# Reordering the head and the normalisation step of a one-core attention kernel: first chunk's copies on ScalarE, other first loads, zeros multiplied on TensorE

## The chip, the cores and the metric

The kernel runs on one core of a Trainium2 chip. The metric is the time of one execution on the device in microseconds (us). Engines are named as in the profile: PE (TensorE matmuls), PEld (its weight loads), DVE (VectorE), ACT (ScalarE), POOL (GpSimd), SP (SyncE, which only issues DMAs here). Lines such as L506 are lines of the kernel before; the changed kernel has its own numbers, about ten higher.

## What is computed

Four sequences of 1024 tokens with 512 features go through a layer norm, an attention with a local window and a compressed sparse part, and a quantised product with a second weight, which is added. In outline:

```
x   = layernorm(hidden)                       # 4 x 1024 x 512
q   = rope(rmsnorm(x @ Wq + bq))              # 16 heads of 128
lk  = rope(rmsnorm(x @ Wlk + blk)),  lv = x @ Wlv + blv
ent = softmax over groups of 4 tokens (x @ Wcmp) weights x     # 256 entries a sequence
ck  = rope(rmsnorm(ent @ Wk + bk)),  cv = ent @ Wv + bv
window part:  softmax(q . lk) over the last 128 tokens, times lv
sparse part:  softmax over the 8 best of q . ck (causal), times cv
out = hidden + (window + sparse) @ Wo + bo + quantised(x) @ quantised(input2)
```

Everything outside the quantised product is in float32.

## The kernel before

**Tiling.** Tokens are handled in 32 chunks of 128, eight to a sequence. A chunk meets the heads in eight units of two heads. So there are 256 units, numbered n = 8 t + u for chunk t and unit u.

**Pipeline.** The main loop goes over slots s. In slot s, PE does the scores of unit s, the query and key products of unit s+3 (`queries`, L478: qp), the output product of s-2 (L797), the values product of s+1 (L581: vp), and the context of s-1 (L764: cp). VectorE and ScalarE do the softmaxes of unit s: `weigh` (DVE L649 to L655 finds the row maxima and the 8 best; ACT L656 and L664 take exponentials), `settle` (DVE L671, L680, L681, L682 masks the sparse part and scales it) and `settle_window` (ACT L687 scales the window part). `normalize(s+2)` (DVE L506, four instructions a unit: th) applies the rms norm to queries and keys; it is the last to read qp, so it frees that PSUM buffer. `squares` (ACT L318) and `spread` (POOL L312, L313: r) make the norm's factor for s+3.

**Rotation.** `rotate` is a generator: POOL's rb product (L332) and DVE's product (L333), then at the second call DVE's subtraction and addition (L335, L336). `normalize` starts it, and `end_rotation` finishes it.

**Two ways to transpose.** From unit 8 on, keys and probabilities are turned by DVE (L556, L559, L705) and a round trip through DRAM (SP issues: qk, qT, lkT, pr, probT; L747 fetches probT in four DMAs). In chunk 0 and for the last unit, PE transposes (tq L534, tp L728), and the results are copied from PSUM: keys by `keep_keys` (ACT L540, DVE L541), probabilities by `keep_turned` (L736: the first of two on ACT, the second on DVE).

**Chunk preparation.** `chunk_prep(t)` is another generator, stepped through labels (A0, B0, A1, ... B7): layer norm (bn_stats on DVE L353, centring on ACT L363, xn on DVE L369), transposes (PE L373), the entries' products (PE L386 yp, L416 ep), their norm (ACT junk_e, POOL er, DVE L437) and rotation (rb_e on POOL; DVE L335, L336), and ck's transpose. For later chunks one label is taken at each `steps()`; the entries are normalised and rotated in unit 5. For chunk 0 the loop drives it by `until` in the slots before slot 0. In chunk 0 too, `fold_first_row` (DVE L269) folds the biases into the weights, and the second weight is quantised in three passes a step.

**Order.** The schedule is written out by hand: each engine executes its instructions in the order of the calls below, and waits where a semaphore says so. qp has a ring of two PSUM buffers of its own; vp, tq, tp, xp, yp, ep and fp share another of two ("pp"). DMAs issued by SP and ACT count on eight completion semaphores in turn, so one waits for the DMA eight before it.

Of the kernel before, what the change touches and what calls it, by code (L numbers as in the profile page):

```python
# [12 lines left out]
F32 = mybir.dt.float32  # L13
# [6 lines left out]
P = 128  # L20
# [18 lines left out]
def kernel(  # L39
# [58 lines left out]
    def load_x(t, purpose):  # L98

        b, c = divmod(t, NCH)  # L100
        xt = work.tile([P, HID], F32, tag="x", name=f"x_{purpose}_{t}")
        nc.sync.dma_start(xt, hidden[b, ts(c, P), :])
        x_tiles[purpose, t] = xt
# [26 lines left out]
    def load_wo(u, engine):  # L130
        engine.dma_start(wo_sb[u], Wo[ts(u, 256), :].rearrange("(h p) n -> p h n", p=P))

    load_x(0, "norm")
    load_wqk(0, nc.sync)
    load_x(1, "norm")
    load_angles(0)

    wkv_sb = const.tile([P, KK, 2 * D + 1], F32, name="wkv_sb")
    nc.sync.dma_start(wkv_sb[:, :, 0:D], Wk.rearrange("(k p) n -> p k n", p=P))
    nc.sync.dma_start(wkv_sb[:, :, D : 2 * D], Wv.rearrange("(k p) n -> p k n", p=P))  # L140
    load_wlv(0, nc.sync)
    load_wqk(1, nc.sync)
    load_angles(1)
    load_wlv(1, nc.sync)
    load_wqk(2, nc.sync)
    load_wlv(2, nc.sync)


    with nc.allow_non_contiguous_dma(reason="512 words once"):
        nc.scalar.dma_start(  # L150
            wkv_sb[:, :, 2 * D : 2 * D + 1], Wcmp.rearrange("(k p) o -> p k o", p=P)
        )
    bias_f = work.tile([P, 1024], F32, tag="probT", name="bias_f", bufs=1)[0:BLK, 0:512]
    nc.vector.memset(bias_f, 0.0)
    nc.scalar.dma_start(bias_f[0:NU, 0:256], bq.rearrange("(u n) -> u n", u=NU))
    nc.scalar.dma_start(bias_f[0:NU, 256:512], blk.rearrange("(u n) -> u n", u=NU))
    bkv_sb = const.tile([NE, 2 * D], F32, name="bkv_sb")
    nc.scalar.dma_start(bkv_sb[:, 0:D], bk.partition_broadcast(NE))
    nc.scalar.dma_start(bkv_sb[:, D : 2 * D], bv.partition_broadcast(NE))
    norm_w = const.tile([P, 2, D], F32, name="norm_w")  # L160
    nc.scalar.dma_start(norm_w[:, 0, :], qn_w.partition_broadcast(P))
    nc.scalar.dma_start(norm_w[:, 1, :], kn_w.partition_broadcast(P))
    blv_n = work.tile([P, 2, P], F32, tag="cT", name="blv_n", bufs=1)[0:NH, 0, :]
    nc.scalar.dma_start(blv_n, blv.rearrange("(h d) -> h d", h=NH))
    bcmp_sb = const.tile([P, 1], F32, name="bcmp_sb")
    nc.scalar.dma_start(bcmp_sb, bcmp.partition_broadcast(P))
    scales = const.tile([P, 2], F32, name="scales")
    nc.scalar.dma_start(scales[:, 0:1], scale.partition_broadcast(P))
    nc.scalar.dma_start(scales[:, 1:2], scale1.partition_broadcast(P))


    nhalf = const.tile([P, 4], F32, name="nhalf")
    nc.vector.memset(nhalf, -0.5)

# [4 lines left out]
    make_identity(nc, ident)  # L179
    ident_b = const.tile([P, P], BF16, name="ident_b")  # L180
    inv = const.tile([P, 1], F32, name="inv")
    bias_b = const.tile([P, 512], BF16, name="bias_b")
    nc.vector.memset(bias_b, 0.0)
    sel = const.tile([P, NU], BF16, name="sel")
    mask_b = const.tile([P, 2 * P + NE], BF16, name="mask_b")
    bo_sb = const.tile([P, HID], F32, name="bo_sb")
# [133 lines left out]
    def rotate(th, cs, nh, a, name):  # L320

        p = th.shape[0]
        a = a.rearrange("p (h t f) -> p h t f", h=nh, t=2)
        bb = work.tile([p, nh, 2, HALF], F32, tag=f"ropeb{nh}", name=f"rb_{name}", bufs=1)
        x12 = th[:, :, 0:ROPE].rearrange("p h (t f) -> p h t f", t=2)

        def wide(v):
            return v.unsqueeze(1).unsqueeze(1).to_broadcast([p, nh, 2, HALF])  # L330

        nc.gpsimd.tensor_tensor(bb, x12, wide(cs[:, HALF:ROPE]), ALU.mult)  # L332
        nc.vector.tensor_tensor(a, x12, wide(cs[:, 0:HALF]), ALU.mult)  # L333
        yield
        nc.vector.tensor_tensor(x12[:, :, 0, :], a[:, :, 0, :], bb[:, :, 1, :], ALU.subtract)  # L335
        nc.vector.tensor_tensor(x12[:, :, 1, :], a[:, :, 1, :], bb[:, :, 0, :], ALU.add)  # L336
# [5 lines left out]
    def chunk_prep(t):  # L342
# [14 lines left out]
        if c == 0:  # L357
            nc.gpsimd.memset(cv, 0.0)
        yield "B0"

        off = work.tile([P, 2], F32, tag="off", name=f"off_{t}")
        nc.gpsimd.tensor_scalar(off[:, 0:1], st[:, 6:7], -1.0, None, ALU.mult)
        nc.scalar.activation(  # L363
            xt, xt, AF.Identity, bias=off[:, 0:1], scale=1.0, accum_out=off[:, 1:2]
        )
        nc.gpsimd.tensor_scalar(off[:, 1:2], off[:, 1:2], 1.0 / HID, None, ALU.mult)
        yield "A1"
        xn = scratch(f"xn_{t}")
        nc.vector.tensor_scalar(xn, xt, off[:, 1:2], r, ALU.subtract, ALU.mult)  # L369
        yield "B1"  # L370
        xp = pp(f"xp_{t}")
        for k in range(KK):
# [128 lines left out]
    def normalize(n):  # L501
# [15 lines left out]
        next(w["rotation"])  # L517
        w["th"], w["thb"] = th, thb

    def end_rotation(n):  # L520
        for _ in units[n].pop("rotation"):
            pass
# [13 lines left out]
    def keep_keys(n):  # L536
        w = units[n]
        tq = w.pop("tq").rearrange("p (t g a i) -> p t g a i", t=2, g=2, a=NB)
        qT, lkT = key_tiles(n)
        nc.scalar.copy(qT.rearrange("p a (i g) -> p g a i", g=2), tq[:, 0])  # L540
        nc.vector.tensor_copy(lkT.rearrange("p a (g i) -> p g a i", g=2), tq[:, 1])  # L541

    def key_tiles(n):
        w = units[n]
# [186 lines left out]
    def keep_turned(n):  # L731
        w, g = units[n], len(parts_of(n))
        probT = work.tile([P, 1024], F32, tag="probT", name=f"probT_{n}", bufs=1)
        probT = of_heads(probT, n)
        for h, tp in enumerate(w.pop("tp")):
            (nc.vector.tensor_copy if h else nc.scalar.copy)(  # L736
                probT[:, :, ds(h * g, g), :],
                tp.rearrange("p (g a i) -> p a g i", a=NB, i=BLK),
            )
        w["probT"] = probT  # L740
# [81 lines left out]
    def for_unit(n, *todo):  # L822
        if 0 <= n < NN:
            for f, *more in todo:
                f(n, *more)

    first, rounding = chunk_prep(0), round_w2()
    until(first, "A1")
    nc.vector.tensor_copy(ident_b, ident)
# [5 lines left out]
    for s in range(-3, NN + 2):  # L835
        t, u = place(s)

        if s == -2 or u == 7 and 0 <= t and t + 2 < NT:
            running = [*running[-2:], chunk_prep(t + 2)]
        if u == 3 and 0 <= t < NT:  # L840
            load_x(t, "sum")
        if u == 6 and 0 <= t < NT:
            running = [*running[-2:], chunk_eight(t)]
        if u == 4 and 0 <= t and t + 2 < NT:
            load_x(t + 2, "norm")

        for_unit(s, (scores, 0), (scores, 1))
        for_unit(s - 2, (keep_context,))
        for_unit(s, (weigh, 0), (weigh, 1))
        for_unit(s + 3, (queries,))  # L850
        if s + 1 < NU:
            for_unit(s + 1, (turn_keys_here,))
        for_unit(s, (settle, 0), (settle, 1))
        for_unit(s, (settle_window, 0), (settle_window, 1))
        for_unit(s + 2, (normalize,))
        if by_dma(s):
            turn(s)
        if s < 0:
            until(first, ("B3", "B4", "B6")[s + 3])
        steps()  # L860
        for_unit(s + 3, (squares, (0, 1, 2, 3)), (spread,))
        if s + 1 < NU:
            for_unit(s + 1, (keep_keys,))
        for_unit(s - 2, (to_output,))
        steps()
        for_unit(s + 2, (end_rotation,))
        if s + 2 >= NU:
            for_unit(s + 2, (turn_keys,))
        if s == -1:
            until(first, "B7")  # L870
        for_unit(s + 1, (values_of,))
        if not by_dma(s):
            for_unit(s, (turn_here,))
        for_unit(s - 1, (values,))
        if by_dma(s):
            fetch(s)
        else:
            for_unit(s, (keep_turned,))
        if s + 2 >= NU:
            for_unit(s + 2, (fetch_keys,))  # L880
        for_unit(s + 1, (keep_values,))

        if 0 <= s < NU:
            fold_first_row(s)
        if 0 <= s + 1 < NU:
            load_first_row(s + 1)
        if s < NU:

            if s == -1:
                late_constants()  # L890
                for k in range(KK):
                    nc.scalar.dma_start(w2_raw[k], input2[ts(k, P), :])
            if 0 <= s < KK:
                for _ in range(4):
                    next(rounding, None)
            if 3 <= s + 6 < NU:
                load_wqk(s + 6, nc.scalar)
            if 3 <= s + 4 < NU:
                load_wlv(s + 4, nc.scalar)
            if 0 <= s + 1 < NU:  # L900
                load_wo(s + 1, nc.scalar)
        if u == 6 and 0 <= t and t + 2 < NT:
            load_angles(t + 2)
        units.pop(s - 1 - NU, None)
# [46 lines left out]
```

## Time and profile before

| What | Value |
|---|---|
| Time, median of 3 runs | 2800.16 us (2798.2 to 2800.68) |
| Time of the profiled execution | 2798.32 us |
| Span of the profiled execution | 2796.6 us |
| Granted TensorE clock, mean | 0.994 |
| PE busy | 2735.4 us (98%) |
| DVE, ACT, POOL busy | 2263.3, 1345.1, 842.6 us |
| First scores (slot 0) | 44.25 us |
| Scores of slot 8 | 157.79 us |

The profile is of one execution. The span runs from its first to its last instruction, and the execution's own time lies 1.7 us above it. An engine's busy time is the union of its instructions. The page cuts the span into 40 slices, with a digit for tenths busy. The lists of waits say which engine, at which line, waited, for whom, for how long in all, how many times, and the longest. In rows of instructions, three durations stand as minimum, median and maximum in ns. The letters before and after `<-` are the tiles written and read.

### The profile page before, as it was taken

Reading aid. Unit: us, or ns where it says so; the run is one execution under the profiler, and the core shown is the slowest. Engines: PE = TensorE matmul, PEld = TensorE weight load, DVE = VectorE, ACT = ScalarE, POOL = GpSimd, SP = SyncE. Lnnn points to the kernel's source line nnn. Section 1 sums busy time; section 2 is a strip of 40 time slices with the busy share of each in tenths; the row PEclk is TensorE's granted clock in tenths of the full one; section 3 lists DMA queues with packets and bytes.
Section 4 is the critical chain, followed back from the end, with each engine's and each line's share of the span. In section 5 each row is a group of like instructions: output and inputs, shape, how many; then the busy total and the mean of one; then the engine's idle time right before and its main releaser. Section 6 shows DMA issues by size and latency. Waiting matters only on the chain.

```text
span 2796.6 us, 48466 instructions
## 1 busy us (share of the span) xinstructions
PE 2735.4 (98%) x12721; PEld 1856.4 (66%) x12721; DVE 2263.3 (81%) x9171; ACT 1345.1 (48%) x5170; POOL 842.6 (30%) x1225
## 2 busy tenths in 40 slices
PE   5799999999999999999999999999999999999998
PEld 3566666676666666666666666666666666666765
DVE  4687888888877788888888787888888878888886
ACT  2345544445455554444445455454444545544443
POOL 2333332233332333322233322333223333222321
PEclk9899999999999999999999999999999999999999
DMA  6345445555544545555554454555555444455554
GB/s 203 98 119 139 136 136 155 154 154 154 146 125 139 139 141 141 154 152 152 153 142 134 132 140 138 152 155 145 153 149 143 129 139 139 136 152 161 145 150 125
DMA packets 623187, 401.96 MB, mean 144 GB/s; under 512 B 307152, under 2 KB 576320, under 8 KB 622912
## 3 DMA queue, kind: packets, MB, share of 16 engines
q1 hardware_dynamic: 610688, 385.29, 50.2%
q10 hardware_dynamic: 12224, 13.56, 1.6%
q8 instruction: 104, 1.70, 0.3%
q14 instruction: 171, 1.40, 0.2%
HBM read 214.64 MB, written 184.03 MB: 143 GB/s over the span
## 4 chain that ended last, share of the span: by engine, by line
PE 92%; DVE 2%; DMA 1%; issue 0%; SPq 0%; ACT 0%; POOL 0%; DVEq 0%; ACTq 0%; POOLq 0%
PE qp L478 30%; PE op L797 15%; PE vp L581 15%; PE cp L764 14%; PE sc L626 5%; PE sc L616 4%; PE sc L623 4%; PE yp L386 2%; PE fp L458 1%; PE ep L416 1%; PE xp L373 0%; DVE wqk L269 0%; DMA probT<-pr 0%; PE sc L627 0%; DVE th L506 0%
## 5 line engine op out<-in xcount | busy, mean ns | idle before, releaser
L478 PE MATMUL qp<-wqk,xnT 128*128 128x512 f32 x2048 | 944.7, 604 | 2.8 <-issue 2.1
L332 POOL TENSOR_TENSOR rb<-th,cs 128x256 f32<-128x256 f32 x256 | 248.1, 969 | 1673.7 <-DVE th L506 1673.7
L478 PEld LDWEIGHTS qp<-wqk,xnT 128*128 128x128 f32 x2048 | 370.3, 191 | 382.9 <-issue 371.7
L581 PEld LDWEIGHTS vp<-wlv,xnT 128*128 128x128 f32 x2048 | 393.0, 192 | 181.6 <-issue 115.8
L581 PE MATMUL vp<-wlv,xnT 128*128 128x256 f32 x2048 | 490.9, 383 | 17.9 <-DVE lkT L541 13.6
L656 ACT ACTIVATE prob<-sc,neg 128x256 f32<-128x256 f32 (+1 forms) x512 | 235.6, 460 | 550.9 <-DVE taken L655 540.4
L797 PE MATMUL op<-wo,cT 128*128 128x512 f32 x1024 | 488.0, 599 | 0.5 <-ACT cT L779 0.5
L649 DVE CUSTOM_DVE_ANT_0 sc<-sc,mask_b 128x256 f32<-128x256 f32 (+1 forms) x512 | 208.0, 406 | 279.8 <-PE sc L627 279.6
L593 ACT COPY lv<-vp 128x256 f32<-128x256 f32 x256 | 95.2, 372 | 471.6 <-PE cp L764 412.7
L687 ACT ACTIVATE prob<-prob,tot 128x256 f32<-128x256 f32 (+1 forms) x512 | 252.4, 493 | 129.1 <-DVE tot L681 127.8
L797 PEld LDWEIGHTS op<-wo,cT 128*128 128x128 f32 x1024 | 186.4, 190 | 189.4 <-issue 129.2
L764 PE MATMUL cp<-probT,lv 128*128 128x128 f32 x1920 | 300.7, 277 | 6.3 <-DMA probT<-pr 5.7
L318 ACT ACTIVATE junk<-qp 128x128 bf16<-128x128 f32 x1024 | 279.7, 273 | 33.1 <-PE qp L478 5.0
L506 DVE SCALAR_TENSOR_TENSOR th<-qp,r,norm_w 128x128 f32<-128x128 f32 x1024 | 286.8, 343 | 5.7 <-ACT junk L318 3.2
L764 PEld LDWEIGHTS cp<-probT,lv 128*128 128x128 f32 x1920 | 275.5, 193 | 23.4 <-issue 10.3
L705 DVE STREAM_TRANSPOSE probB<-prob 128x512 f32<-128x512 f32 (+2 forms) x494 | 281.9, 608 | 0.0
L313 POOL TENSOR_TENSOR r<-r,nhalf 128x4 f32<-128x4 f32 x256 | 260.5, 1018 | 21.3
L764 PE MATMUL cp<-probT,cv 128*128 128x128 f32 x1536 | 257.1, 277 | 0.0
L626 PE MATMUL sc<-ckT,qT 128*128 128x96 f32 (+7 forms) x1024 | 226.3, 303 | 0.0
L764 PEld LDWEIGHTS cp<-probT,cv 128*128 128x128 f32 x1536 | 214.8, 194 | 0.0
L623 PE MATMUL sc<-lkT,qT 128*128 128x128 f32 x1024 | 207.9, 285 | 0.0
L779 ACT ACTIVATE cT<-cp,blvT 128x128 f32<-128x128 f32 x512 | 160.0, 364 | 92.7 <-PE cp L764 83.4
(130 smaller groups left out, 3802.1 us busy)
## 6 DMA issues: line engine op xcount, KB each, us to landing
pr<-probB SPq DMA_DIRECT2D x127, 512.0 KB, 2.6
probT<-pr SPq DMA_DIRECT2D x508, 128.0 KB, 2.9
qk<-thb SPq DMA_DIRECT2D x992, 64.0 KB, 1.8
pr<-probB SPq DMA_DIRECT2D x96, 384.0 KB, 2.3
probT<-pr SPq DMA_DIRECT2D x384, 96.0 KB, 2.4
qT<-qk SPq DMA_DIRECT2D x248, 128.0 KB, 2.9
lkT<-qk SPq DMA_DIRECT2D x248, 128.0 KB, 2.8
x_norm<-_attn_hidden_states_dram SPq DMA_DIRECT2D x32, 256.0 KB, 3.0
```

The lines of the kernel that those rows point to most:

```text
L313: nc.gpsimd.tensor_tensor(r, r, nhalf[: ss.shape[0], 0:n], ALU.pow)
L318: nc.scalar.activation(junk[: src.shape[0]], src, AF.Square, accum_out=acc)
L332: nc.gpsimd.tensor_tensor(bb, x12, wide(cs[:, HALF:ROPE]), ALU.mult)
L478: nc.tensor.matmul(qp, xnT[:, k if k or not t else KK, :], wqk_sb[u][:, k, :], start=(k == 0), stop=(t > 0 and k == KK - 1),)
L506: nc.vector.scalar_tensor_tensor(th[:, i, :], qp[:, ts(i, D)], r[:, i : i + 1], norm_w[:, i // 2, :], ALU.mult, ALU.mult,)
L581: nc.tensor.matmul(vp[:, 0:256], xnT[:, k, :], wlv_sb[u][:, k, :], start=(k == 0), stop=(k == KK - 1),)
L623: nc.tensor.matmul(blocks(sc[:, P : 2 * P]), q, lkT[:, :, ds(h * BLK, BLK)], start=True, stop=True)
L626: nc.tensor.matmul(sc[:, spa], q, ckT[:, 0:m], start=True, stop=False)
L687: nc.scalar.mul(prob[:, loc], prob[:, loc], tot[:, 0:1])
L705: nc.vector.transpose(pb[:, :, ds(h * g, g), :], prob[:, parts[0] * P : (parts[-1] + 1) * P].rearrange("p (g b i) -> p b g i", b=NB, i=BLK),)
L764: nc.tensor.matmul(blocks(cp[:, h, :]), v, probT[:, :, h * len(parts) + i - parts[0], :], start=(i == parts[0]), stop=(i == parts[-1]),)
L797: nc.tensor.matmul(op, cT[:, h, :], wo_sb[u][:, h, :], start=(u == 0 and h == 0), stop=(u == NU - 1 and h == 1),)
```

## The change

1. **First loads.** SP's order becomes x0, Wq and Wlk of unit 0, Wk, Wv, Wq and Wlk of unit 1, angles 0, x1, Wq and Wlk of unit 2, three times Wlv, angles 1. ACT's DMAs start with the biases; blv and the two scales are issued in slot -2 (`late_loads`).
2. **First layer norm.** In chunk 0, xn is made on DVE straight from mean and factor; the centring pass on ACT and the two POOL instructions around it remain for later chunks.
3. **Zeros on PE.** Twelve bf16 matmuls of a zero tile (128x128 by 128x512) stand first in PE's queue.
4. **Copies on ACT.** The second copy of keys and that of probabilities in chunk 0 move from DVE to ACT; the probabilities' copy of the last unit too.
5. **Order within a slot.** `normalize(s+2)` moves ahead of `settle` in every slot. Its rotation's POOL product stays with it, and DVE's product of the rotation follows after `settle_window` (`go_on_rotating`). In chunk 0 the keys' transposes move ahead of the queries.
6. **First entries.** In slots -3 to -1 the preparation of chunk 0 is driven further (B3, A6, B6 instead of B3, B4, B6) and placed ahead of `normalize`; in slot -1, vp stands ahead of the last step.

```diff
+    load_x(0, "norm")
+    nc.vector.memset(bias_f, 0.0)
+
+    nc.scalar.dma_start(bias_f[0:NU, 0:256], bq.rearrange("(u n) -> u n", u=NU))
+    nc.scalar.dma_start(bias_f[0:NU, 256:512], blk.rearrange("(u n) -> u n", u=NU))
     load_wqk(0, nc.sync)
-    load_x(1, "norm")
-    load_angles(0)
...
+    load_wqk(1, nc.sync)
+    load_angles(0)
...
+    load_x(1, "norm")
+    load_wqk(2, nc.sync)
+    load_wlv(0, nc.sync)
+    load_wlv(1, nc.sync)
+    load_wlv(2, nc.sync)
+    load_angles(1)
+
+    def late_loads():
+        nc.scalar.dma_start(blv_n, blv.rearrange("(h d) -> h d", h=NH))
+        nc.scalar.dma_start(scales[:, 0:1], scale.partition_broadcast(P))
+        nc.scalar.dma_start(scales[:, 1:2], scale1.partition_broadcast(P))
+
+    bias_b = const.tile([P, 512], BF16, name="bias_b")
+    nc.vector.memset(bias_b, 0.0)
...
         nc.gpsimd.tensor_tensor(bb, x12, wide(cs[:, HALF:ROPE]), ALU.mult)
+        yield
         nc.vector.tensor_tensor(a, x12, wide(cs[:, 0:HALF]), ALU.mult)
         yield
...
+        xn = None
+        if t:
...
+        else:
+            xn = scratch(f"xn_{t}")
+            nc.vector.tensor_scalar(xn, xt, st[:, 6:7], r, ALU.subtract, ALU.mult)
         yield "A1"
...
+    def go_on_rotating(n):
+        next(units[n]["rotation"])
+
...
-        nc.vector.tensor_copy(lkT.rearrange("p a (g i) -> p g a i", g=2), tq[:, 1])
+        nc.scalar.copy(lkT.rearrange("p a (g i) -> p g a i", g=2), tq[:, 1])
...
-            (nc.vector.tensor_copy if h else nc.scalar.copy)(
+            nc.scalar.copy(
...
+    warm = pp("warm")
+    for _ in range(12):
+        nc.tensor.matmul(warm, bias_b[:, 0:P], bias_b, start=True, stop=True)
+
...
         for_unit(s, (weigh, 0), (weigh, 1))
+        if 0 <= s < NU - 1:
+            for_unit(s + 1, (turn_keys_here,))
         for_unit(s + 3, (queries,))
-        if s + 1 < NU:
+        if s < 0:
             for_unit(s + 1, (turn_keys_here,))
+            until(first, ("B3", "A6", "B6")[s + 3])
+        for_unit(s + 2, (normalize,))
         for_unit(s, (settle, 0), (settle, 1))
         for_unit(s, (settle_window, 0), (settle_window, 1))
-        for_unit(s + 2, (normalize,))
+        for_unit(s + 2, (go_on_rotating,))
         if by_dma(s):
             turn(s)
-        if s < 0:
-            until(first, ("B3", "B4", "B6")[s + 3])
         steps()
...
+        for_unit(s + 1, (values_of,))
         if s == -1:
             until(first, "B7")
-        for_unit(s + 1, (values_of,))
...
+            if s == -2:
+                late_loads()
             if s == -1:
                 late_constants()
```

More of the change, by code (lines that the diff above doesn't have):

```diff
@@ L131, in load_wo @@
         engine.dma_start(wo_sb[u], Wo[ts(u, 256), :].rearrange("(h p) n -> p h n", p=P))
+    wkv_sb = const.tile([P, KK, 2 * D + 1], F32, name="wkv_sb")
+    bias_f = work.tile([P, 1024], F32, tag="probT", name="bias_f", bufs=1)[0:BLK, 0:512]
+    bkv_sb = const.tile([NE, 2 * D], F32, name="bkv_sb")
+    norm_w = const.tile([P, 2, D], F32, name="norm_w")
+    bcmp_sb = const.tile([P, 1], F32, name="bcmp_sb")
+    scales = const.tile([P, 2], F32, name="scales")
+    blv_n = work.tile([P, 2, P], F32, tag="cT", name="blv_n", bufs=1)[0:NH, 0, :]
     load_x(0, "norm")
+    nc.vector.memset(bias_f, 0.0)
+    nc.scalar.dma_start(bias_f[0:NU, 0:256], bq.rearrange("(u n) -> u n", u=NU))
+    nc.scalar.dma_start(bias_f[0:NU, 256:512], blk.rearrange("(u n) -> u n", u=NU))
     load_wqk(0, nc.sync)
-    load_x(1, "norm")
-    load_angles(0)
[L138 to L146, printed above, removed]
     with nc.allow_non_contiguous_dma(reason="512 words once"):
@@ L152 @@
         )
[L153 to L157, printed above, removed]
+    nc.sync.dma_start(wkv_sb[:, :, 0:D], Wk.rearrange("(k p) n -> p k n", p=P))
+    nc.sync.dma_start(wkv_sb[:, :, D : 2 * D], Wv.rearrange("(k p) n -> p k n", p=P))
+    nc.scalar.dma_start(norm_w[:, 0, :], qn_w.partition_broadcast(P))
+    nc.scalar.dma_start(norm_w[:, 1, :], kn_w.partition_broadcast(P))
+    nc.scalar.dma_start(bcmp_sb, bcmp.partition_broadcast(P))
+    load_wqk(1, nc.sync)
+    load_angles(0)
     nc.scalar.dma_start(bkv_sb[:, 0:D], bk.partition_broadcast(NE))
     nc.scalar.dma_start(bkv_sb[:, D : 2 * D], bv.partition_broadcast(NE))
[L160 to L169, printed above, removed]
+    load_x(1, "norm")
[10 more added lines that the diff above has]
+    nc.vector.memset(bias_b, 0.0)
     nhalf = const.tile([P, 4], F32, name="nhalf")
@@ L181 @@
     inv = const.tile([P, 1], F32, name="inv")
-    bias_b = const.tile([P, 512], BF16, name="bias_b")
-    nc.vector.memset(bias_b, 0.0)
     sel = const.tile([P, NU], BF16, name="sel")
@@ L359, in chunk_prep @@
         yield "B0"
[L361 to L366, printed above, removed]
+        xn = None
+        if t:
+            off = work.tile([P, 2], F32, tag="off", name=f"off_{t}")
+            nc.gpsimd.tensor_scalar(off[:, 0:1], st[:, 6:7], -1.0, None, ALU.mult)
+            nc.scalar.activation(
+                xt, xt, AF.Identity, bias=off[:, 0:1], scale=1.0, accum_out=off[:, 1:2]
+            )
+            nc.gpsimd.tensor_scalar(off[:, 1:2], off[:, 1:2], 1.0 / HID, None, ALU.mult)
+        else:
+            xn = scratch(f"xn_{t}")
+            nc.vector.tensor_scalar(xn, xt, st[:, 6:7], r, ALU.subtract, ALU.mult)
         yield "A1"
-        xn = scratch(f"xn_{t}")
-        nc.vector.tensor_scalar(xn, xt, off[:, 1:2], r, ALU.subtract, ALU.mult)
+        if t:
+            xn = scratch(f"xn_{t}")
+            nc.vector.tensor_scalar(xn, xt, off[:, 1:2], r, ALU.subtract, ALU.mult)
         yield "B1"
```

## The prediction

> **What bounds the kernel now.** I read the page first, then busy time by stretches of the span, then the waits of the first 200 us and of 300 to 2700 us apart.
>
> ```profile
> span 2796.6 us, 48466 instructions
> ...
> PE 2735.4 (98%) x12721; PEld 1856.4 (66%) x12721; DVE 2263.3 (81%) x9171; ACT 1345.1 (48%) x5170; POOL 842.6 (30%) x1225
> ...
> PE   5799999999999999999999999999999999999998
> ...
> PEclk9899999999999999999999999999999999999999
> ```
>
> TensorE is the bound. Only the first two slices are thin, and there the granted clock dips too. By stretches (length, busy us of PE, PEld, DVE, ACT, POOL, then clock, DMA):
>
> ```profile
> 0.00:20.00 20.00, 6.97 (x11) 3.21 (x12) 6.10 (x18) 2.68 (x4) 4.49 (x19) 1.00 0.80 234
> 20.00:40.00 20.00, 11.43 (x36) 5.58 (x34) 7.03 (x26) 6.33 (x32) 6.80 (x14) 0.92 0.59 187
> 100.00:120.00 20.00, 14.66 (x55) 10.21 (x55) 13.31 (x44) 6.43 (x27) 6.88 (x8) 0.83 0.30 79
> 200.00:2740.00 2540.00, 2539.20 (x11885) 1725.52 (x11884) 2097.21 (x8560) 1255.34 (x4815) 764.44 (x1111) 1.00 0.53 145
> 2740.00:2797.00 57.00, 45.62 (x232) 33.01 (x230) 36.10 (x131) 19.77 (x66) 11.01 (x12) 0.95 0.40 115
> ```
>
> Between 200 and 2740 us PE idles 0.8 us of 2540. Nothing can be won there, only lost; about 50 of the 61 us without PE work lie before 180 us. What ended the waits there:
>
> ```profile
> PE xp L373 <- DVE xn L369: 12.3, 1, 12.3
> PE vp L581 <- DVE lkT L541: 13.6, 4, 5.3
> PE tp L728 <- DVE lkT L541: 10.1, 3, 4.5
> ACT probT L736 <- PE cp L764: 25.9, 7, 6.7
> DVE probT L736 <- ACT probT L736: 20.5, 6, 5.7
> ```
>
> So PE waits 12.3 us for the first tokens and 23.7 us for VectorE's key copies in chunk 0.
>
> **Start.** Before: x lands at 3.87; the centring on ACT waits for its own DMA issues until 9.22, so xn is written at 11.70 to 12.29 and qp0 starts at 14.14. PE is cold: qp's slow matmuls take 1.22 us against 0.59, and qp0 lasts until 20.5. After: bn_stats and r from POOL come at about 5.7, xn (0.59) ends at 6.35, xp and the xnT copy end by 9. qp0 starts at about 9.2: Wlk0, which landed at 8.13 beside the x1 load, sets no later time. The twelve zero matmuls at 0.43 us each (cold f32 matmuls of this width start 0.86 apart, and a bf16 one takes half as long: 0.22 against 0.43 in the warm rows) fill 1.75 to 6.9 us and delay nothing: xn comes at 6.35. Here rule and row differ. In this trace PE went slow after pauses of 3.6 us or more and needed 3.2 to 5.6 us to recover, about 8 us at the first start; the Trainium skill ("TensorE: Matmul & The Clock Gate", "What's actually happening") gives about 3.4 us of sustained work. By the rule qp0 is at full speed; by the first start its first 0.6 us is not, +0.3 us. I take the rule, with the 0.3 in the range. Then, with rows of before: qp1 14.7 to 18.4, first-entry sums (ep) to 19, normalisation of unit 0 to 21.05, which frees qp's buffer, qp2 to 24.85, vp0 to 27.0, entry rotation, ACT Identity of chunk 1 to 28.8, squares, q and lk copies on ACT to 30.95. The first scores start at 31.5 instead of 44.25: **-12.7** (+-2). The three loads put off to slot -2 stand on ACT's queue (about 0.4 us an issue) before work that waits for PE.
>
> **Chunk 0, slots 0 to 7.** Before, VectorE ends a slot with lkT (0.42), two rotation products, then waits for PE's tp and ACT's copy (20.5 us in 6), then probT (0.42), the fold of the first row (2.28) and three quantising passes (0.45 each); so weigh of the next slot comes 2.2 to 4.5 us after its scores. With both copies on ACT the fold runs while PE does vp and tp. I added each engine's rows in its order, with the waits. For the order before this gives 14.2, 17.5, 15.3, 17.5, 16.0, 12.2, 11.9, 9.3 us for the slots, against 13.9, 17.4, 14.7, 18.6, 15.6, 12.2, 11.9, 9.2 in the trace. For the new order: 12.0, 16.4, 10.6, 13.1, 10.9, 15.2, 9.8, 9.4. Slots 2 to 4 give 4 to 5 us each. Slot 5 loses 3, as the entry rotation waits for ACT's squares, which now follow two copies more; slot 1 gives 1 (VectorE's memset waits for ACT's xnT copy). ACT takes 16 x 0.4 = 6.4 us more in 97, of which slot 5 shows the part on the path. Moving tq ahead of the queries costs PE nothing. **-16.3.** Bounds: 23.7 us of named waits plus 5 recoveries of 1.8 us (vp 3.5 against 1.73) is 33 at most; slots 2 and 6 alone, 6 at least.
>
> **Tail.** The last unit's second copy also goes to ACT, in line after the first: **+0.4**.
>
> **Every slot: normalize ahead of settle.** This is the part that meets the full stretch. VectorE does as much work, but ACT's window products (they wait for settle), and all behind them on ACT, come later by the four th (1.11 us). And POOL's rb, which starts at the end of th, now runs beside settle. Rows (count: min/median/max ns):
>
> ```profile
> L332 POOL TENSOR_TENSOR rb<-th,cs x227: 962/969/977, 300.4 to 2698.5; 128x256 f32<-128x256 f32 x114
> L671 DVE SCALAR_TENSOR_TENSOR prob<-taken,prob x512: 176/315/1123, 50.3 to 2779.4; 128x32 f32<-128x32 bf16 x22, 128x128 f32<-128x128 bf16 x22, 128x224 f32<-128x224 bf16 x22, 128x64 f32<-128x64 bf16 x21
> L336 DVE TENSOR_TENSOR th<-thb,rb x226: 265/283/1370, 304.5 to 2690.2; 128x128 f32<-128x128 f32 x113
> ```
>
> The maxima are VectorE instructions held up by a POOL instruction: 0.19 became 1.12, and in 31 slots (unit 6, under POOL's quantising) 0.28 became 1.37. rb itself lasts 0.97, of which it waits 0.38 for L333 and holds 0.59. The Trainium skill ("SBUF — State Buffer", "SBUF: two separate sides") says that the pair of ports is an exclusive lock, held for the whole instruction, against VectorE instructions with two SBUF inputs or in a two-port mode. L671, L680 and L682 are such, the stream transposes that rb lies beside today are none. So it speaks against this change: settle's first instruction goes first (0.25), rb takes its 0.59, and L680 waits, some 0.45 us a slot. No row shows rb against settle. Bounds: 0 to 0.6; I take 0.45, as the rows above obey the rule.
>
> What of it reaches PE? In most slots nothing: probT lands 2 to 4 us before cp. The tight place is unit 6 of each chunk:
>
> ```profile
> DVE kv L335 <- POOL rb_e L332: 35.2, 29, 1.2
> DVE kv L437 <- POOL er L313: 13.1, 29, 0.8
> ...
> PE cp L764 <- DMA probT<-pr: 0.3, 1, 0.3
> ```
>
> In slot 5 VectorE waits for the entry rotation. In the slot from 971.4 us: th 975.70 to 976.82; ACT's window products end 976.08, then the cv copy, junk_e and the four squares until 978.48; POOL er to 978.75, r 978.84 to 980.12, rb_e to 980.41; VectorE weighs unit 86 at 981.86. In the new order ACT is 1.11 + 0.45 = 1.56 later, squares end at 980.04, r ends at 981.36 and rb_e at 981.67: 1.26 later, and so is weigh. The settle of that slot adds its 0.45: probT(6) is 1.7 us later. Its spare time, from the four transfers' completions to cp, is 0.13 to 2.3 us over the 31 chunks, mean 0.63, and 0.13 is what remains when PE just waits (cp 86 starts at 999.25, its last packets end at 999.1). The sum of max(0, 1.7 - spare) over 31 chunks is **37.6**. Unit 5 (spare about 0.95) bears its 0.45 in nearly every chunk, and the few stalls there spare unit 6 as much. Unit 7 (about 2) and the next chunk's first keys (0.84) are as late, but PE has by then been held 1.2 us, so they add nothing. Rounded down for that: **+36**. With rb holding nothing the delay is 0.76 and the sum **+11**; with 0.6 in both places, 2.0 and **+46**.
>
> **Sum.** -12.7 - 16.3 + 0.4 + 36 = +7.4. The profiled execution is its span 2796.6 + 1.7 = 2798.3; the median of the runs is 2800.16, 1.9 above. 2798.3 + 7.4 + 1.9 = 2807.6, or 2807.
>
> **Rivals.**
> (A) The forecast: the start gains 29, each chunk returns about 1.2 us in slot 7. Own range 2797 to 2818.
> (B) Faster: rb slips in between settle's short instructions, or VectorE's delay is absorbed. The break-even is 29 / 31 = 0.92 us a chunk; at +11 the time is 2800.2 - 17.6 = 2782. For it: VectorE has 19% idle and waits 250 us for PE scores in the stretch, so most slots have room. Against: that room isn't in slots 5 and 6, where it waits for POOL.
> (C) Slower by more: the stall comes as in A or worse, and ACT, which has to copy keys and probabilities in order, holds weigh's exponentials in chunk 0, so that its slots give 6 and not 16. Then 2800.2 + 17.7 = 2818; with +46, 2828. For it: in the trace ACT's probT already waits 25.9 us for cp, and everything behind it would wait.
> (D) The zeros don't warm PE, or the load order doesn't bring x sooner. The first costs up to 3 us (qp0 6.4 against 3.5), the second at most the 12.7. It moves A to 2810 or 2820, and is in its range and C's.
>
> **Chances.** A 0.55, B 0.28, C with D's worse end 0.17. About 0.2% (5.6 us) is what a measurement of this kernel can tell from no change: 2794.6 to 2805.8. B lies below it but for 0.03; of A 0.13 falls within and 0.01 below; C lies above. Faster 0.26, within 0.16, slower 0.58. The range takes in A, most of B and C: 2779 to 2828.
>
> **What would show it.** Right: first scores near 31.5 us and cp of unit 7 near 129; PE waits for probT about 1.2 us in each of 31 chunks (PE busy in 200 to 2740 near 2502); VectorE's wait for rb_e near 1.9 each instead of 1.2; L680 or L671 with a median up by 0.3 to 0.5 in one head of two; PE's waits for lkT gone. Wrong: L680's median unchanged beside rb (then B), PE still full between 200 and 2740 us, or the first scores after 36 us.

## The result and the profile after

The changed kernel takes 2788.98 us (median, 2787.32 to 2790.94) against 2799.77 us for the kernel before beside it: a ratio of 0.9962, with an interval of 0.9951 to 0.9972. It is 10.8 us faster. The forecast was 2807 us and slower. The profiled execution has a span of 2785.8 us.

From the page of the changed kernel:

```profile
span 2785.8 us, 48890 instructions
...
PE 2741.0 (98%) x12733; PEld 1849.1 (66%) x12733; DVE 2318.1 (83%) x9154; ACT 1366.3 (49%) x5185; POOL 795.9 (29%) x1223
...
PE   7999999999999999999999999999999999999998
...
PEclk8999999999999999999999999999999999999999
...
L776 PE MATMUL cp<-probT,lv 128*128 128x128 f32 x1920 | 301.6, 277 | 18.1 <-DMA probT<-pr 15.5
...
L692 DVE TENSOR_SCALAR tot<-tot 128x2 f32<-128x2 f32 x512 | 195.4, 382 | 17.7
```

The second slice of PE is full now. L776 is L764 of before: the context product, which stood idle for 6.3 us before, stands for 18.1 us here. L692 was L680: its mean over the whole execution was 177 ns and is 382. Busy time by stretches (length, then busy us of PE, PEld, DVE, ACT and POOL, granted clock, DMA share, GB/s):

```profile
0.00:20.00 20.00, 15.73 (x41) 7.44 (x42) 7.23 (x24) 3.83 (x12) 3.27 (x17) 0.91 0.85 254
20.00:40.00 20.00, 14.52 (x44) 8.26 (x43) 9.88 (x42) 5.41 (x26) 8.73 (x18) 0.75 0.78 234
100.00:120.00 20.00, 19.17 (x90) 12.33 (x89) 18.07 (x69) 11.44 (x49) 9.65 (x8) 1.00 0.40 93
200.00:2740.00 2540.00, 2524.97 (x11766) 1707.49 (x11765) 2143.24 (x8482) 1260.90 (x4770) 713.43 (x1103) 1.00 0.54 144
```

PE does more in the first 120 us, and it now has holes in the long stretch: 15.0 us of 2540, against 0.8. The starts of scores tell the same story by stage. Slot 0 starts at 34.78 us instead of 44.25 (9.5 us won), slot 16 at 207.33 instead of 241.39 (34.1 us won so far), and the context of unit 255 at 2777.5 instead of 2788.2. So 10.8 us are left: **23.3 us were given back in the long stretch, about 0.8 us a chunk.** The holes show only 15.0 us of it, because the profile models the ends of matmuls and a short wait can disappear under them. By the starts, the step from the last values product (vp) to the first context product (cp) grew by 17.8 us in slots 6 and 7 of 29 chunks, and the other six slots kept their length within 0.03 us.

The waits of the first 200 us, and those of 300 to 2700 us (engine and line, what ended the wait, us in all, times, longest):

```profile
ACT probT L748 <- PE cp L776: 14.0, 7, 3.3
...
PE vp L593 <- ACT lkT L553: 5.5, 2, 3.8
...
PE tp L740 <- ACT lkT L553: 2.1, 2, 1.2
```

```profile
PE cp L776 <- DMA probT<-pr: 11.4, 19, 1.5
PE cp L776 <- issue: 2.2, 6, 0.8
```

```profile
DVE kv L338 <- POOL rb_e L334: 51.7, 28, 2.1
...
DVE kv L446 <- POOL er L315: 12.8, 25, 0.9
```

PE's 23.7 us of waits for the keys' copies in chunk 0's slots became 7.6. (Ahead of slot 0, at the transpose of the first entries, PE waits 3.6 us for a key copy, where before it waited 4.6 us for the entries.) In the long stretch PE waits for probT, and VectorE waits 1.85 us each time for rb_e (51.7 in 28), where it was 1.2.

Three rows, again from 300 to 2700 us, show settle's second instruction before (L680) and after (L692), and POOL's rb, which now runs beside it:

```profile
L680 DVE TENSOR_SCALAR tot<-tot x452: 168/169/380, 308.0 to 2696.6; 128x2 f32<-128x2 f32 x151
...
L692 DVE TENSOR_SCALAR tot<-tot x448: 168/171/694, 305.6 to 2697.1; 128x2 f32<-128x2 f32 x150
...
L334 POOL TENSOR_TENSOR rb<-th,cs x224: 717/735/842, 305.5 to 2695.3; 128x256 f32<-128x256 f32 x112
```

A median of 171 ns and a mean of 382 mean that half of the instructions are held up: one head of two, by about 0.43 us. In the slot from 942.99 us, for example, rb runs from 4.34 to 5.06 us after the scores and L692 of the first head from 4.47 to 5.09; that of the second head takes 0.17.

### The profile page after: what moved, and what is told of

It is laid out like the page before. It is cut to its first block, busy times and chain, and to the rows that moved or that the text cites. A ratio compares the mean times of both kernels' runs of the same rounds, so it can differ in the third digit from the quotient of the medians.

```text
span 2785.8 us, 48890 instructions
## 1 busy us (share of the span) xinstructions
PE 2741.0 (98%) x12733; PEld 1849.1 (66%) x12733; DVE 2318.1 (83%) x9154; ACT 1366.3 (49%) x5185; POOL 795.9 (29%) x1223
## 5 line engine op out<-in xcount | busy, mean ns | idle before, releaser
L334 POOL TENSOR_TENSOR rb<-th,cs 128x256 f32<-128x256 f32 x256 | 193.6, 756 | 1023.0 <-DVE th L515 1023.0
L776 PE MATMUL cp<-probT,lv 128*128 128x128 f32 x1920 | 301.6, 277 | 18.1 <-DMA probT<-pr 15.5
L776 PEld LDWEIGHTS cp<-probT,lv 128*128 128x128 f32 x1920 | 271.0, 192 | 45.0 <-issue 31.0
L776 PE MATMUL cp<-probT,cv 128*128 128x128 f32 x1536 | 256.0, 276 | 0.0
L776 PEld LDWEIGHTS cp<-probT,cv 128*128 128x128 f32 x1536 | 213.5, 193 | 0.0
L692 DVE TENSOR_SCALAR tot<-tot 128x2 f32<-128x2 f32 x512 | 195.4, 382 | 17.7
L314 POOL TENSOR_SCALAR r<-ss 128x4 f32<-128x4 f32 x256 | 60.0, 235 | 516.3 <-ACT junk L320 511.1
```

What stands on the lines that cost most here:

```text
L776: nc.tensor.matmul(blocks(cp[:, h, :]), v, probT[:, :, h * len(parts) + i - parts[0], :], start=(i == parts[0]), stop=(i == parts[-1]),)
```

## The experiments

Theory 1 says: the head wins 34 us, and normalising ahead of settle costs 23 us later, at units 5 and 6 of each chunk, through two things: POOL's rb holds up settle ("the port" below), and ACT's window products wait for settle and so come later by the four th. Rivals: the order is neutral; the loss is spread over the slots; one of the two things makes the loss alone.

### Where the loss is made

`head_only`: the old order from slot 8 on.

```diff
-        for_unit(s + 2, (normalize,))
+        early = s < NU
+        if early:
+            for_unit(s + 2, (normalize,))
         for_unit(s, (settle, 0), (settle, 1))
         for_unit(s, (settle_window, 0), (settle_window, 1))
+        if not early:
+            for_unit(s + 2, (normalize,))
         for_unit(s + 2, (go_on_rotating,))
```

> The changed kernel, with the order of the kernel before (settle, window product, then normalise with its rotation products) in all slots from 8 on; chunk 0 keeps the new order. Theory 1: of the changed kernel's traces, 34 us are won up to slot 16 and 23 us given back afterwards, by normalising ahead of settle. Then this gives 2789 - 23 = 2766 us (2761 to 2771), and PE has no waits for probT between 300 and 2700 us. Rival 2: the loss after slot 16 comes from elsewhere (later transfers, the state the head leaves behind), and the order is neutral: 2785 to 2791 us.

Measured: 2762.89 us (2762.7 to 2764.8), ratio 0.9868 (0.9854 to 0.9881). The stretch of 200 to 2740 us and PE's only wait in 300 to 2700 us:

```profile
200.00:2740.00 2540.00, 2535.55 (x11880) 1726.65 (x11879) 2099.84 (x8534) 1254.61 (x4798) 764.48 (x1108) 1.00 0.54 145
```

```profile
PE cp L776 <- DMA probT<-pr: 0.2, 1, 0.2
```

The changed kernel without this one edit is 26 us faster, and faster than both kernels compared here.

`norm_only`: the kernel before with this edit alone, from slot 8 on (`early = s >= NU`).

> The kernel before, with only one edit: from slot 8 on, normalise and POOL's rotation product stand ahead of settle, DVE's rotation product after it. Theory 1: 23 us slower than before, 2823 us (2818 to 2828), with DVE's L680 at 0.6 us in one head of two. Rival 2 (the order is neutral): 2800 us. My forecast's sizes would give 2836.

Measured: 2823.83 us, ratio 1.0084 (1.0070 to 1.0098): 24.4 us slower. The edit costs about the same from both sides (26 and 24 us), so the head has no part in the loss.

`late_in_5_6`: `early = s < NU or u not in (5, 6)`.

> The changed kernel, with the old order only in slots of units 5 and 6; six slots of eight keep normalise ahead of settle and with it the hold-up of settle by POOL. Theory 1: the loss is made in those two slots alone, through the entries' rotation and probT(5), probT(6): 2766 to 2770 us. Rival 3: the loss is spread over all slots (0.43 us of DVE each, which adds up in the slack of transfers): a quarter of it goes, 2783 us.

Measured: 2763.64 us (2763.18 to 2764.01), the same as `head_only`. It lies a little below its range. Six slots of eight may normalise first at no cost. The loss is made in slots 5 and 6: VectorE waits for the entries in slot 5, and the loads of probT with the least time to spare are those of units 5 and 6. No run takes the two slots apart.

### What makes it: the port or ACT's delay

`rb_late`: rb issued behind settle in the program's order.

```diff
-        nc.gpsimd.tensor_tensor(bb, x12, wide(cs[:, HALF:ROPE]), ALU.mult)
         yield
+        nc.gpsimd.tensor_tensor(bb, x12, wide(cs[:, HALF:ROPE]), ALU.mult)
```

> The changed kernel, with POOL's rotation product rb put after settle, beside DVE's own rotation product as in the kernel before; the four th stay ahead of settle. This takes away the hold-up of settle and leaves ACT's delay by th. Theory 1 with the port held as half of the cause: ACT's window products come 0.94 us later than before instead of 1.37, weigh of unit 6 about 0.5 later instead of 0.88; the loss falls from 23 to some 6 us, 2772 us (2768 to 2777), L692 back at 0.17 us in all. Rival 4: only the order on DVE and ACT matters: 2787 to 2789 us.

Measured: 2788.28 us, unchanged, but this does not speak for the rival, since the edit did not do what it was meant to. POOL has an order of its own, and nothing stands in it between the two places; rb waits for th alone and runs beside settle as ever (rb takes 737 ns in the median, 735 in the changed kernel, and the row of L692 has nearly the same 168/171/691 ns).

`rb_held`: the same, with a wait that holds.

```diff
+        if nh > 1:
+            yield
+            nc.vector.memset(bb[:, 0, 0, 0:1], 0.0)
         nc.gpsimd.tensor_tensor(bb, x12, wide(cs[:, HALF:ROPE]), ALU.mult)
-        yield
```

> The changed kernel, with POOL's rb held back: a small DVE memset of one element a partition in rb's tile stands behind settle and the window product, and rb waits for it. (In the kernel rb_late the edit moved rb only within POOL's own order, where nothing stood between, and rb still ran beside settle.) Theory 1a (the port is half of the cause): L692 back at 0.17 us, window products 0.95 later than before instead of 1.37, weigh of unit 6 at about 2.1 us after the scores instead of 2.49: 2772 us (2767 to 2778). Rival 4 (ACT's delay by the four th alone makes the loss): 2784 to 2789 us.

Measured: 2769.05 us (2767.93 to 2772.37), ratio 0.9892 (0.9879 to 0.9906): 20 of the 26 us are back, though normalise still stands first. L694 is L692 here; the rows of 300 to 2700 us:

```profile
L336 DVE MEMSET rb<- x225: 59/59/59, 304.1 to 2692.4; 128x1 f32 x113
...
L694 DVE TENSOR_SCALAR tot<-tot x450: 168/169/171, 302.5 to 2691.7; 128x2 f32<-128x2 f32 x150
```

The hold-up is gone to the last instruction.

`norm_held`: `norm_only` with the same memset.

> The kernel before with normalise ahead of settle from slot 8 on (as in norm_only, which took 24 us more), and rb held back behind settle by a one-element DVE memset, as in rb_held. What is left is ACT's delay by the four th. From rb_held's time against head_only's: +6 us, 2806 us (2803 to 2808). From its trace (10.9 us lost after slot 16): +10 us, 2810 us. If the port had no part: 2822 us or more.

Measured: 2802.93 us, ratio 1.0014 (1.0007 to 1.0020): 3.8 us slower, against 24.4 us with the port held. PE's wait for probT in 300 to 2700 us fell from 12.9 us in `norm_only` to this:

```profile
PE cp L770 <- DMA probT<-pr: 1.7, 4, 1.1
```

It lies just below its range of 2803 to 2808. So the hold-up makes 20 us of the loss, from either side. The 4 to 6 us that are left go with the place of th: ACT's window products still end 0.94 us later (5.73 to 6.67 in the table below). That this delay makes them is argued; no run moves it alone. In the trace of `rb_held` the division is less sharp, 12 and 11 us after slot 16, but its execution, 2772.37 us, was the slowest of the four. The times decide, since they agree from both sides.

Times in us after the first scores of unit 5 or 6, means over 29 chunks, from the traces ("turned" is the end of the transposes on VectorE that make probB; "landed" is the completion of the last of the four loads):

| | before | after | rb_held |
|---|---|---|---|
| unit 5: settle ends | 5.46 | 6.84 | 6.42 |
| unit 5: window products end | 5.73 | 7.10 | 6.67 |
| unit 5: DVE has turned the probabilities | 8.02 | 8.25 | 7.87 |
| unit 5: SP issues the first probT load | 13.72 | 14.57 | 14.14 |
| unit 6: weigh starts | 1.61 | 2.49 | 2.06 |
| unit 6: probabilities turned | 8.65 | 9.75 | 8.90 |
| unit 6: probT has landed | 18.51 | 19.61 | 18.82 |
| length of slots 6 and 7 together | 20.61 | 21.37 | 20.89 |

### What the head's parts are worth

Six of these undo one part of `head_only` (2763 us), so that a loss is what the part brings while the others stay; `ho_more_zeros` adds to it, and the last two start from the kernel before. The parts depend on each other, so the losses do not add up to the whole.

`ho_dve_copies`: keys' and probabilities' second copies back on VectorE.

> head_only with the second copies of keys and probabilities (chunk 0 and the last unit) back on VectorE. If these copies make most of the 22.8 us won in chunk 0's slots: slots 2 to 4 lengthen by 3 to 5 us each, 2775 to 2783 us. Rival (the slots are shorter because the keys' transposes and normalise come earlier): 2763 to 2767 us.

Measured: 2789.58 us: 26.7 us lost, beyond the range expected. Slots 0 to 7 last 117 us instead of 91. The waits of 36 to 126 us show the old picture again:

```profile
DVE probT L748 <- ACT probT L748: 15.4, 5, 4.5
...
DVE lkT L553 <- ACT qT L552: 10.9, 6, 2.6
```

`ho_tq_late`: keys' transposes behind the queries in chunk 0.

```diff
+        for_unit(s + 3, (queries,))
         if 0 <= s < NU - 1:
             for_unit(s + 1, (turn_keys_here,))
-        for_unit(s + 3, (queries,))
```

> head_only with chunk 0's key transposes behind the queries, as in the kernel before. In the forecast this order costs PE nothing. If the earlier transposes let ACT copy keys before the squares and so bring the next scores: slots lengthen by 1 to 3 us each, 2770 to 2780 us. Rival (the copies wait for their place in ACT's order anyway): 2762 to 2764 us.

Measured: 2782.01 us (2780.57 to 2783.82): 19 us lost. The reason is not the one in the expectation, and the forecast that this order costs PE nothing does not hold beside an early normalise. From the waits of 36 to 126 us:

```profile
DVE th L515 <- PE tq L546: 20.8, 6, 5.1
```

Normalise writes th, of which there is one buffer, and the transposes read the old one. With normalise first on VectorE and the transposes late on PE, VectorE stands for these 20.8 us ahead of all of settle.

`norm_old`: `early = s < 0`, so that normalise stands behind settle in chunk 0 too.

> The changed kernel with normalise behind settle in all slots from 0 on, chunk 0 too. If the hold-up of settle by rb costs chunk 0 what it costs a slot (0.4 us) and nothing is won by the earlier normalise: 2760 to 2763 us. Rival (the earlier normalise frees qp's buffer in time for the queries, and chunk 0's slots owe part of their 24 us to it): 2765 to 2772 us.

Measured: 2765.11 us (2764.3 to 2766.97), 2.2 us above `head_only`, in the range of the rival. In its trace the slots up to 16 gain 22.5 us instead of 24.2, so the earlier normalise brings up to 2 us in chunk 0; its start, with the same instructions, was 2.6 us later than that of `head_only`, which is the scatter of the clock that the last section shows.

`ho_act_norm`: chunk 0's layer norm by the pass on ACT. `ho_old_loads`: the first loads as before. `ho_no_zeros`: without the twelve zero matmuls. `ho_more_zeros`: ten more of them between the first transposes and qp0.

> head_only with chunk 0's layer norm as before: centring on ACT between two POOL instructions, in the new order of loads. If the direct layer norm is what brings the first tokens early: ACT is free of DMA issues only at about 7.6 us, its table load and pass end at 10, xn at 10.9, qp0 at about 12.8 instead of 9.5: 2766 to 2767 us. Rival (the loads alone do it, or qp0 is bound by its weights): 2763 to 2764 us.

> head_only with the first loads in the order of the kernel before, on both queues, blv and scales included. If the loads bring the gain at the start together with the direct layer norm: ACT is free of its issues at 9.2 us instead of 7.6, so xnT's copy ends near 11 instead of 9.5, qp0 starts 1.5 us later, and wqk_1, which lands at 19.4, holds up qp1 by 2 to 3 us: 2765 to 2768 us. Rival (the direct layer norm alone brings it): 2763 us.

> The fastest kernel so far (head_only, 2763 us) without the twelve zero matmuls. If they warm the clock for qp0: the first transposes and qp0 run at half speed as before the change, qp0 takes 6.4 us instead of 3.5 to 5.2, and the time is 2764.5 to 2766.5 us. Rival (the clock falls back in the pause of 2.5 us between the transposes and qp0, and other waits absorb the rest): 2763 us within 1.

> head_only with ten more zero matmuls between chunk 0's first transposes and qp0, where PE stands idle for 2.5 us in every profile so far. If it is this pause that lets the clock fall back in some executions (qp0 5.2 us in two profiles, 3.5 in two): qp0 takes 3.5 us in all, 2761.5 to 2763 us with a narrower spread. Rival (the clock's state at qp0 is set by other things): 2763 us, spread as before.

| | us | first scores | qp0 |
|---|---|---|---|
| head_only | 2762.89 (2762.7 to 2764.8) | 31.79 | 9.47 to 13.0 |
| ho_act_norm | 2766.94 (2764.9 to 2770.1) | 37.40 | 11.98 to 17.4 |
| ho_old_loads | 2766.28 (2765.2 to 2768.8) | 36.15 | 11.01 to 16.2 |
| ho_no_zeros | 2765.67 (2762.6 to 2768.2) | 35.31 | 9.46 to 15.3 |
| ho_more_zeros | 2764.31 (2761.7 to 2765.5) | 31.44 | 9.41 to 13.1 |

The last two columns are of one profiled execution each. Layer norm and loads bring about 4 and 3 us. The zeros bring at most 3: the ranges of the two times overlap. More zeros bring nothing that can be told apart.

`copies_only`: the kernel before with the two copies on ACT.

```diff
-        nc.vector.tensor_copy(lkT.rearrange("p a (g i) -> p g a i", g=2), tq[:, 1])
+        nc.scalar.copy(lkT.rearrange("p a (g i) -> p g a i", g=2), tq[:, 1])
...
-            (nc.vector.tensor_copy if h else nc.scalar.copy)(
+            nc.scalar.copy(
```

> The kernel before with one edit: both second copies of chunk 0 and the last unit on ACT. If the copies alone make the 24 us won in chunk 0's slots: 2775 us (2773 to 2779). Rival (they need the keys' transposes ahead of the queries, as otherwise PE's vp and tp still wait for the keys' copy): 2783 to 2795 us.

Measured: 2775.03 us (2773.26 to 2777.64), ratio 0.9913 (0.9899 to 0.9926): 24.2 us faster with two calls changed.

`copies_tq`: the same, with the keys' transposes ahead of the queries.

> The kernel before with the copies on ACT and chunk 0's key transposes ahead of the queries. Both readings expect the slots' whole gain here, 24 us: 2775 us (2773 to 2779). If it stays above 2780, the earlier start or normalise has a part in the slots' gain.

Measured: 2775.62 us, the same. So the copies make the whole of the slots' gain. The transposes' place brings nothing by itself, but an early normalise in chunk 0 needs it, as `ho_tq_late` shows.

## Why the prediction was wrong

The sides of the sum were right in kind and wrong in size, and the sign hung on the difference.

- **Start, -12.7.** The profile after has first scores at 34.78 us (-9.5). In the eight profiles with the same zeros, loads and layer norm they lie from 31.16 to 34.78, so the forecast's 31.5 is at the fast end. The steps came as worked out: xn ended at 6.17 us (6.35 forecast), the transposes started at 6.48, qp0 at 9.58 (9.2 forecast). What varied is the clock. The forecast took from the Trainium skill ("TensorE: Matmul & The Clock Gate", "What's actually happening") that about 3.4 us of sustained work bring full speed, so that qp0 would have it. In half of the profiles it did not, which cost 1.7 us at qp0 and, in the profile after, as much again at qp2, where 0.3 had been allowed. The step that failed is that the zeros were counted and the pause of 2.5 us behind them was not; the last section shows what it did.
- **Chunk 0, -16.3.** Measured -24.6 up to slot 16, of which 22.8 are in slots 0 to 7; here 6.5 us were missed. The forecast for slot 5 was 15.2 us and it took 11.1; slot 3, 13.1 against 11.1. The step that failed is "slot 5 loses 3, as the entry rotation waits for ACT's squares". The wait came: just ahead of slot 5 VectorE stands 3.4 us, where before it stood 0.9. From the waits of 36 to 126 us of the changed kernel:

```profile
DVE kv L338 <- POOL rb_e L334: 1.8, 1, 1.8
DVE kv L446 <- POOL er L315: 1.5, 1, 1.5
```

  It made the slot's weigh start 2.5 us after its scores, against 0.6 to 0.9 in slots 2 to 4, but PE then stood for only 0.8 us. So the wait was right and its cost was not: most of it never reached PE. `copies_only` has 90.9 us for slots 0 to 7, so the 22.8 us are the copies' own. The hole in PE at 178.67 us of before (1.7 us) did not come back either, but that is not the copies' doing: `copies_only` still has it (1.9 us).
- **Tail, +0.4.** No run separates it; the stages leave nothing for it to explain.
- **The port, 0.45 us a slot.** Measured 0.43. The rule of the Trainium skill ("SBUF — State Buffer", "SBUF: two separate sides"), that the ports which VectorE and POOL share are held for a whole instruction, held for this pair: a VectorE instruction of 0.17 us lasted until POOL's ended. With the memset in between, none did.
- **Every slot, +36.** Measured +23.3 by the trace, +24 to +26 by the times. The place (probT of unit 6, through rb_e and the entries), the sign and the wait of VectorE (1.9 forecast, 1.85 measured) were right. The step that failed is "probT(6) is 1.7 us later". It was 1.10 later. Of the 0.6 us missing, 0.38 lie in "1.26 later, and so is weigh" (0.88 measured), and 0.22 in "the settle of that slot adds its 0.45" (8.65 to 9.75 is 1.10, of which 0.88 came in with weigh). Two things make up most of this. First, the four th take as long as ever (1.12 us in all of these traces), but they delay settle by only 0.96 us, as `rb_held` shows (5.46 to 6.42), not by 1.11: settle starts 1.03 us after the first th, where the rotation's product, which reads th, started 1.15 after it, and head 1's part of settle starts 0.21 us instead of 0.29 after the start of head 0's last instruction. So "VectorE does as much work" was wrong by 0.15 us, and the turned probabilities of unit 5 come that much earlier in `rb_held` than before. Second, the delay was read off one slot of one chunk: in that chunk weigh came 1.09 us later, and over the 29 chunks 0.64 to 1.17.
- **What the forecast did not see:** "Unit 5 bears its 0.45 in nearly every chunk". Its probabilities are turned only 0.23 us later, but probT(5) is issued 0.85 us later, and its median spare time, from landing to cp, fell from 1.04 us to 0.20, where about 0.13 remain when PE just waits. SP issues in order, and ahead of that load stand the writes of unit 7's keys (qk), which wait for the delayed entry rotation. SP's issues for one unit 5, before (11.3 and 13.2 us after the scores) and after (12.4 and 14.3):

```profile
981.96 1.79 SPq L564 DMA_DIRECT2D qk<-thb  x4
983.86 1.83 SPq L747 DMA_DIRECT2D probT<-pr  x4
```

```profile
955.38 1.78 SPq L576 DMA_DIRECT2D qk<-thb  x4
957.27 1.82 SPq L759 DMA_DIRECT2D probT<-pr  x4
```

  Slot 6 grew by 0.26 us, slot 7 by 0.50. With the measured delays of 0.93 and 1.10 us, the forecast's own sum over the 31 chunks gives 20.7 us, near the 23.3; unit 6 alone gives 19.8, since what PE loses to unit 5 spares unit 6 as much. So unit 5 changes where PE stands more than how long, and the size of the delay is what the forecast had wrong.
- **The sum.** Forecast +7.4, measured -10.8. Of the 18 us between them the long stretch makes 12.7 and chunk 0 8.3; the start, 3.2 us less than forecast in this profile, goes the other way.
- **Rivals.** Rival B had the sign, and the loss stayed under the break-even of 0.92 us a chunk (0.8). But its mechanism, a rb that slips in between, did not happen. The bound for rb holding nothing, +11, is what `rb_held` shows by its trace; by its time it is +6.

The working range of 2797 to 2818 for the likeliest case treated two terms of about 30 us as if their difference were known within 10.

## What to carry to other kernels

When one engine is full, ask of every reordering elsewhere which transfer has the least spare time per period, and test the order only there: here two slots of eight decided 26 us. A POOL instruction that is moved can hold up what VectorE does beside it: here 0.43 us beside settle, and nothing beside the stream transposes of the probabilities (686 ns in the mean beside rb before, 687 without it after, at 128x512). Move it by a real dependency: a new place in the program text moved nothing where POOL's own queue had nothing in between. A change that bundles gains and losses is worth taking apart: two copies gave 24 us, and leaving out one edit made the whole 36 us faster than the kernel before.

## What was not expected of the hardware

- The zeros held the clock only in half of the executions, and the traces show on what it hung. In all 17 profiles of this case the granted clock is full or half, and it changes only on a grid of 3.41 us, which lies elsewhere against the kernel's start in each execution. Steps of this grid around the pause, first in the profile after, then in `head_only` (the second column is the length, the third what PE was busy, and the clock stands before the last two):

```profile
6.08:9.49 3.41, 1.00 (x7) 0.57 (x5) 0.70 (x4) 1.83 (x2) 1.38 (x7) 1.00 0.75 166
9.49:12.91 3.42, 3.33 (x4) 1.51 (x5) 3.10 (x9) 0.04 (x1) 0.00 (x0) 0.50 0.84 254
```

```profile
4.43:7.84 3.41, 2.05 (x11) 0.84 (x9) 0.78 (x3) 0.30 (x1) 2.58 (x11) 1.00 0.80 218
7.84:11.25 3.41, 1.78 (x4) 0.87 (x5) 2.81 (x7) 1.56 (x2) 0.00 (x0) 1.00 0.86 239
```

  In the profile after, the pause of 2.5 us falls into one step of the grid, in which PE works 1.00 us of 3.41, and the next step runs at half speed. In `head_only` the grid cuts the pause in two, both steps hold more work, and the clock stays. The eight profiles agree: qp0 took 5.2 us in the four in which such a step held 1.00 to 1.24 us of work, and 3.5 in the four in which none held less than 1.57. The edge is not shown more closely: the later pauses of 1.84 us in the profile after (21.07 to 22.91) and 1.83 us in `head_only` (19.63 to 21.46) each left 1.6 us of work in their step, and the first was followed by 3.4 us at half speed, the second was not.
- In the profile of `ho_more_zeros` the pause is filled, and qp0 runs at full speed; one profile does not show that it always does, and its times are not better.
- Without the zeros qp0 took 5.8 us, 2.3 us more than the best. The first scores of the eight profiles scatter by 3.6 us, about twice the 1.7 us of one half-speed start, since qp2 can have one too.
